# Transposes in place of matrix products with permutation matrices, in a stack of four graph layers

## The chip, the cores and the metric

The kernel runs on one core of a Trainium2 chip. The metric is the time of one execution on the device, in microseconds (us). TensorE multiplies matrices, VectorE (DVE in the profile), ScalarE (ACT) and GpSimd (POOL) work on what it leaves, and DMA engines move data between memory and the core. TensorE takes one operand as weights, loaded beforehand (PEld in the profile), streams the other one past it (PE), and writes to PSUM, from where DVE or ACT copies the result.

## The reference

Sixteen graphs with N = 1024 nodes and D = 256 features, all in fp32, pass through four layers. Each layer normalises its input, applies ReLU, runs one graph operation with the adjacency matrix and adds the result to its input:

```
h = relu(layernorm(x)); x = x + layer_0(h, adj)   # attention with mask adj
h = relu(layernorm(x)); x = x + layer_1(h, adj)   # normalised adjacency
h = relu(layernorm(x)); x = x + layer_2(h, adj)   # node by node, gated
h = relu(layernorm(x)); x = x + layer_3(h, adj)   # sum of neighbours, MLP
```

Layers 0, 1 and 3 are large products. Layer 2 is sequential: a scan over the nodes,

```
def step(h, i):
    x = h_e[:, i];  x_par = row_i(norm_adjT) @ h
    r, z = split(sigmoid(x @ W_ioux.T + b + x_par @ W_iouh.T + b'))
    hc = tanh(x @ W_coux.T + ... + (x_par * r) @ W_couh.T + ...)
    h[:, i] = z * x_par + (1 - z) * hc
```

so the value of node i depends on the new values of its neighbours with a smaller index.

## The kernel before

**Order.** Each graph's nodes are cut into NT = 8 blocks of P = 128. Within a block the kernel does not follow the nodes' own order. It looks for an order in which nodes that do not depend on one another stand together, in 8 groups of S = 16, and works on a group of all 16 graphs at once. What layer 2 reads must therefore be permuted, and most of it also transposed. Both happen in one product on TensorE: for a block of data A (128 by 128) and a permutation matrix `to`, the product of A as weights and `to` as the moving operand is A transposed, with its columns in the new order. `to` is made on VectorE by comparing the row `step` (0 to 127) with each node's `place` (L413, L600).

**Layers 0 and 1** run in one loop over the graphs (`layers_0_1`). The work of layer 0 on graph i, of layer 1 on graph i−1 and two kinds of side work are recorded side by side: the order of nodes (`orders`, on VectorE) and, from the tenth turn of the loop on, `put_in_order(b)` for one or two graphs a turn. The order in which each engine then takes the instructions is set by a scheduler, which works from its own costs of instructions. The sums of both layers are L290; their four results per layer are copied from PSUM at L293 and L295; the small products that follow are L360 and L391.

`put_in_order(b)` is a generator in six parts, and has all but one of the changed lines:

- It loads two diagonals of blocks of the adjacency (`ad`), a column of blocks (`ab`) and the layer's input (`h2`), makes `to`, and masks and scales `ad` and `ab` on GpSimd (L416 to L421).
- L429: 16 products (2 halves c of the features, 8 blocks t) turn `h2` into `hT`. Four of them fill one PSUM tile `pt` of 512 columns, of which there are two; ACT (c = 0, L432) or DVE (c = 1, L434) copies it out. Then `hT` goes to memory as `heT_d` (L436).
- L443 and L445: 15 products turn the blocks of `ad` into `ao`, which takes the same single buffer as `hT` (L438, name "hT"). Its copies (L450 on ACT, L452 on DVE) so wait until `heT_d` is written. L454 and L455 write `ao` to memory.
- L458 sums eight products with `ab` into `bs` (scaled at L460), and L464 turns its two halves, which L466 copies and L467 writes as `base_d`.

This makes 16 × (16 + 15 + 2) = 528 products with a permutation.

**Layer 2** has its order on TensorE, VectorE, ScalarE and GpSimd written out by hand. It goes through the blocks t and their 8 groups s. Each group takes one or more rounds (`round_`; K = `KS[s]` of them: 1, 1, 1, 1, 1, 2, 2, 4), a chain of products at L784, four transposes at L816 with the identity, and gates on ACT and DVE. Between the steps of that chain `fill` puts tasks for later groups and for the next block, by weights and costs written in the code. One of these is the sum over the other blocks (`task` in `base_tasks`, L616, copied and scaled on ACT at L603); at its end `turn` takes the sum, turns its two halves with `to` (L630) and copies them to `bxt` (L631). The planner's cost of `turn` is 0.44. It runs for 16 graphs and 7 blocks: 224 products. Its PSUM tile `pf` is one of three, which the tasks of L616, L666, L737 and L765 use too.

Two places use `nc.tensor.transpose` already: L816 and, in layer 3, L1118.

Of the kernel before, what the change touches and what calls it, by code (L numbers as in the profile page):

```python
# [16 lines left out]
P = 128  # L17
# [22 lines left out]
def gnn_stack(ctx: ExitStack, tc: tile.TileContext, a: dict, out: bass.AP):  # L40
    nc = tc.nc
# [29 lines left out]
    def rows(ap):  # L71
        return ap.rearrange("(t p) d -> p t d", p=P)
# [155 lines left out]
    def layers_0_1():  # L228
        with ExitStack() as st:
# [68 lines left out]
            at, q, g, h1, h2, dis = {}, {}, {}, {}, {}, {}  # L298
# [101 lines left out]
            def put_in_order(b):  # L400


                ad = big.tile([P, NT, 2 * P], F32, name="ad")
                nc.sync.dma_start(ad[:, 0, P:], a["adjT"][b, :P, :P])
                nc.sync.dma_start(ad[:, 1:], bass.AP(tensor=a["adjT"].tensor, offset=a["adjT"].offset + b * N * N + P * N,
                                                     ap=[[N, P], [P * N + P, NT - 1], [1, 2 * P]]))
                ab = big.tile([P, NT, P], F32, name="ab")
                nc.sync.dma_start(ab, rows(a["adj"][b])[:, :, :P])
                if b not in h2:
                    h2[b] = big.tile([P, NT, D], F32, name="h2", bufs=2)  # L410
                    nc.sync.dma_start(h2[b], rows(he_d[b]))
                to = big.tile([P, NT, P], F32, name="to")
                nc.vector.tensor_tensor(to, step[:, None].to_broadcast([P, NT, P]),  # L413
                                        place.rearrange("i (t b) -> i t b", b=B)[:, :, b : b + 1].to_broadcast([P, NT, P]),
                                        ALU.is_equal)
                nc.gpsimd.affine_select(out=ad[:, :, P:], in_=ad[:, :, P:], compare_op=ALU.is_gt, fill=0.0, base=0,  # L416
                                        pattern=[[0, NT], [-1, P]], channel_multiplier=1)
                nc.gpsimd.affine_select(out=ab[:, 0], in_=ab[:, 0], compare_op=ALU.is_ge, fill=0.0, base=0,
                                        pattern=[[-1, P]], channel_multiplier=1)
                nc.gpsimd.tensor_tensor(ad[:, :, P:], ad[:, :, P:], dinv[:, b][:, :, None].to_broadcast([P, NT, P]), ALU.mult)  # L420
                nc.gpsimd.tensor_tensor(ad[:, 1:, :P], ad[:, 1:, :P],  # L421
                                        dinv[:, b, 1:][:, :, None].to_broadcast([P, NT - 1, P]), ALU.mult)
                yield
                hT = big.tile([P, DC, N], F32, name="hT")
                for c in range(DC):
                    for t0 in range(0, NT, 4):
                        pt = psum.tile([P, 512], F32, name="pt")
                        for t in range(4):
                            nc.tensor.matmul(pt[:, t * P : (t + 1) * P], h2[b][:, t0 + t, c * P : (c + 1) * P], to[:, t0 + t],  # L429
                                             start=True, stop=True)  # L430
                        if c == 0:
                            nc.scalar.copy(hT[:, c, t0 * P : (t0 + 4) * P], pt)  # L432
                        else:
                            nc.vector.tensor_copy(hT[:, c, t0 * P : (t0 + 4) * P], pt)  # L434
                    if c == DC - 1:
                        nc.gpsimd.dma_start(heT_d[b], hT)  # L436
                    yield
                ao = big.tile([P, NT, 2 * P], F32, name="hT")  # L438
                nc.gpsimd.memset(ao[:, NT - 1, P : P + S], 0.0)
                for t0 in range(0, NT, 2):  # L440
                    pt = psum.tile([P, 2, 2, P], F32, name="pt")
                    for t in (t0, t0 + 1):
                        nc.tensor.matmul(pt[:, t - t0, 0], ad[:, t, P:], to[:, t], start=True, stop=True)  # L443
                        if t + 1 < NT:
                            nc.tensor.matmul(pt[:, t - t0, 1], ad[:, t + 1, :P], to[:, t + 1], start=True, stop=True)  # L445
                    n = 4 * P if t0 + 2 < NT else 3 * P
                    got = ao[:, t0 : t0 + 2].rearrange("p t n -> p (t n)")[:, :n]
                    pt = pt.rearrange("p t k n -> p (t k n)")[:, :n]
                    if t0 % 4 == 0:
                        nc.scalar.copy(got, pt)  # L450
                    else:
                        nc.vector.tensor_copy(got, pt)  # L452
                        yield
                nc.gpsimd.dma_start(near_d.rearrange("(t b j) n -> b j t n", t=NT, b=B)[b], ao[:, :, : P + S])  # L454
                nc.gpsimd.dma_start(next_d[b].rearrange("t j n -> j t n"), ao[:, : NT - 1, P + S :])  # L455
                pb = psum.tile([P, 512], F32, name="pt")
                for j in range(NT):
                    nc.tensor.matmul(pb[:, :D], ab[:, j], h2[b][:, j], start=j == 0, stop=j == NT - 1)  # L458
                bs = small.tile([P, D], F32, name="bo", bufs=1)
                nc.scalar.activation(bs, pb[:, :D], AF.Copy, scale=dinv[:, b, 0:1])  # L460
                yield
                pt = psum.tile([P, 512], F32, name="pt")
                for c in range(DC):
                    nc.tensor.matmul(pt[:, c * P : (c + 1) * P], bs[:, c * P : (c + 1) * P], to[:, 0], start=True, stop=True)  # L464
                bo = small.tile([P, DC, P], F32, name="bo", bufs=1)
                nc.vector.tensor_copy(bo, pt[:, :D].rearrange("p (c i) -> p c i", c=DC))  # L466
                nc.gpsimd.dma_start(base_d[b], bo)  # L467
                del h2[b]
                yield
# [10 lines left out]
            for i in range(B + 2):  # L480
# [3 lines left out]
                for b in when.get(i, ()):  # L484
                    if b < i - 2:
                        del h2[b]
                    job = put_in_order(b)
                    next(job)
                    jobs += [lambda job=job: next(job)] * 6
# [52 lines left out]
    def layer_2(shared, early):  # L542
        with ExitStack() as st:
# [32 lines left out]
            def base_tasks(t, bxt):  # L576
# [20 lines left out]
                def summed(b, pb):  # L597
                    if b not in state:
                        to = big.tile([P, P], F32, name="to")
                        nc.vector.tensor_scalar(to, step, place[:, t * B + b : t * B + b + 1], None, op0=ALU.is_equal)  # L600
                        state[b] = [to]
                        bs = big.tile([P, D], F32, name="bs")
                        nc.scalar.activation(bs, pb, AF.Copy, scale=dinv[:, b, t : t + 1])  # L603
                        state[b].append(bs)
# [19 lines left out]
                def turn(b, held):  # L624
                    def run():
                        summed(b, held[0])
                        to, bs = state.pop(b)
                        pt = psum.tile([P, DC, P], F32, name="pf", bufs=3)
                        for c in range(DC):
                            nc.tensor.matmul(pt[:, c], bs[:, c * P : (c + 1) * P], to, start=True, stop=True)  # L630
                        return lambda: nc.vector.tensor_copy(bxt[:, :, b], pt)  # L631
                    return 0.44, run

# [235 lines left out]
            with tc.manual_schedule(engines={mybir.EngineType.PE, mybir.EngineType.DVE, mybir.EngineType.Activation, mybir.EngineType.Pool}):  # L869
# [17 lines left out]
                for t in range(NT):  # L887
# [10 lines left out]
                    for s in range(NS):  # L898
# [36 lines left out]
                        for c in range(DC):  # L935
                            to = x[:, c].rearrange("p (b i) -> p b i", b=B)
# [282 lines left out]
```

## Time and profile before

| | |
|---|---|
| time, median of 3 runs | 4941.66 us (4936.22 to 4944.18) |
| span of the profiled execution | 4950.9 us |
| mean granted clock of TensorE | 0.978 |
| put_in_order runs in | 751 to 1545 us |
| layer 2 runs in | 1545 to about 3500 us, `turn` from 1592 to 3270 |
| layer 3's main part runs in | about 3500 to 4951 us |

The profile's page lists each engine's busy time first and then the costliest groups of instructions. In a group, "out<-in" names the tiles, "x512" counts the instructions, the two numbers after the bar are the busy time in us and the mean duration of one in ns, and what follows is the engine's idle time ahead of them and what ended it. Matmuls overlap in the pipeline, so the busy time of a group divided by its count, or the distance between starts in the timeline, tells more of their price than the mean duration. The products of the change in this trace:

| line | product | products | matmul instructions | PE busy, us |
|---|---|---|---|---|
| L429 | hT from h2 | 256 | 512 | 64.6 |
| L443 | ao from ad, own block | 128 | 256 | 54.1 |
| L445 | ao from ad, next block | 112 | 224 | 45.3 |
| L464 | base from bs | 32 | 64 | (median 275 ns each) |
| L630 | turn | 224 | 448 | 76.0 |

### The profile page before, as it was taken

To read this page: it belongs to the slowest core of one execution; us is meant where nothing else is said; L and a number is where in the kernel's file an instruction comes from. 1 tells how busy PE (TensorE), PEld (TensorE's weight loads), DVE (VectorE), ACT (ScalarE), POOL (GpSimd) and SP (SyncE) were. 2 spreads that over 40 slices of the span, in tenths; PEclk is the share of its full clock that TensorE was granted. 3 is DMA by queue.
4 is the path that set the end of the run, shared out by engine and by line. 5 is a ranking of instruction groups with operands and counts; after the bars stand their busy time and mean duration, and the time that the engine had idled before them with its cause. 6 is when DMAs were issued, how large, how long until landed. Compare 5 with 4: busy or idle time off the path is not lost. (4 is left out here: it accounts for less than half of the span.)

```text
span 4950.9 us, 52564 instructions
## 1 busy us (share of the span) xinstructions
PE 4624.2 (93%) x18431; PEld 3061.1 (62%) x18431; DVE 2388.3 (48%) x6366; ACT 1174.7 (24%) x2388; POOL 1597.7 (32%) x1883
## 2 busy tenths in 40 slices
PE   8998999999997999999999999998799999999999
PEld 4443455565555777777777777776365555555656
DVE  6667754446443454545454445454534434334343
ACT  1111112112111222222222222222222323223232
POOL 3122333334323323323232232332523424234232
PEclk9999999999998999999999999999899999999999
DMA  5333335454535443544343445330422222221200
GB/s 157 116 93 98 95 96 177 165 171 149 186 118 189 142 136 119 158 137 152 122 138 108 146 129 164 123 118 34 149 84 86 77 77 85 77 94 69 84 26 17
DMA packets 530500, 577.13 MB, mean 117 GB/s; under 512 B 41552, under 2 KB 438992, under 8 KB 527824
## 3 DMA queue, kind: packets, MB, share of 16 engines
q1 hardware_dynamic: 499056, 460.79, 29.3%
q0 software_dynamic: 31040, 111.44, 6.3%
q8 instruction: 195, 3.19, 0.3%
q14 instruction: 209, 1.71, 0.1%
HBM read 470.17 MB, written 116.65 MB: 119 GB/s over the span
## 5 line engine op out<-in xcount | busy, mean ns | idle before, releaser
L290 PE MATMUL pa<-at,h 128*128 128x512 f32 x1088 | 492.2, 604 | 29.4 <-DVE ag L295 29.4
L1094 PE MATMUL ph<-ag,w 128*128 128x512 f32 x1024 | 478.9, 611 | 33.9 <-DVE hh L1098 33.9
L1132 PE MATMUL po<-w,hh 128*128 128x256 f32 x2048 | 447.7, 379 | 0.0
L616 PE MATMUL pf<-hb,ab 128*128 128x256 f32 x1568 | 419.4, 387 | 22.0 <-ACT bs L603 18.8
L1132 PEld LDWEIGHTS po<-w,hh 128*128 128x128 f32 x2048 | 387.8, 190 | 59.3 <-issue 7.9
L290 PE MATMUL pa<-at,q 128*128 128x512 f32 x960 | 420.9, 594 | 0.0
L290 PEld LDWEIGHTS pa<-at,h 128*128 128x128 f32 x1088 | 207.9, 194 | 271.4 <-issue 229.3
L1094 PEld LDWEIGHTS ph<-ag,w 128*128 128x128 f32 x1024 | 179.1, 190 | 295.4 <-DVE hh L1098 151.7
L1100 POOL TENSOR_TENSOR ss<-ss,sq 128x512 f32<-128x512 f32 x224 | 302.3, 1349 | 121.8 <-ACT sq L1097 117.4
L983 POOL DMA_INDIRECT hs_d<-h,table x128 | 129.9, 1015 | 621.1 <-DVE gz L739 446.6
L616 PEld LDWEIGHTS pf<-hb,ab 128*128 128x128 f32 x1568 | 284.0, 194 | 73.7 <-ACT bs L603 26.0
L290 PEld LDWEIGHTS pa<-at,q 128*128 128x128 f32 x960 | 179.7, 190 | 224.8 <-issue 220.7
L737 PE MATMUL pf<-wx,hs 128*128 128x512 f32 x512 | 248.0, 626 | 30.8 <-POOL hs L720 25.1
L1098 DVE TENSOR_SCALAR hh<-ph,b 128x512 f32<-128x512 f32 x256 | 190.0, 746 | 154.6 <-ACT sq L1097 120.7
L1079 PE MATMUL pa<-bxt,h 128*128 128x512 f32 x512 | 227.9, 597 | 19.9 <-POOL bxt L1061 19.9
L765 PE MATMUL pf<-bd,h 128*128 128x384 f32 (+5 forms) x768 | 218.8, 373 | 27.1 <-DVE bxt L768 27.1
L827 DVE TENSOR_TENSOR r<-r,x 128x256 f32<-128x256 f32 x230 | 123.6, 559 | 232.7 <-ACT r L826 231.2
L1079 PE MATMUL pa<-at,h 128*128 128x512 f32 x512 | 228.8, 597 | 0.0
L1097 ACT ACTIVATE sq<-ph,b 128x512 f32<-128x512 f32 x224 | 153.4, 685 | 234.2 <-PE ph L1094 189.1
L1124 ACT ACTIVATE hh<-hh,rw 128x512 f32<-128x512 f32 x256 | 168.4, 712 | 138.7 <-DVE hh L1123 136.7
L1135 DVE TENSOR_TENSOR x<-x,po 128x256 f32<-128x256 f32 x120 | 50.4, 420 | 289.0 <-PE po L1132 288.9
L1079 PEld LDWEIGHTS pa<-bxt,h 128*128 128x128 f32 x512 | 97.3, 191 | 137.1 <-issue 115.1
(233 smaller groups left out, 7948.3 us busy)
## 6 DMA issues: line engine op xcount, KB each, us to landing
at<-in_adjT SPq DMA_DIRECT2D x64, 1024.0 KB
ab<-in_adj SPq DMA_DIRECT2D x128, 512.0 KB
bxt<-in_adjT SPq DMA_DIRECT2D x64, 512.0 KB
at<-in_adjT SPq DMA_DIRECT2D x64, 512.0 KB
ad<-in_adj SPq DMA_DIRECT2D x128, 128.0 KB
x_d<-x POOLq DMA_DIRECT2D x16, 1024.0 KB
he_d<-h POOLq DMA_DIRECT2D x16, 1024.0 KB, 9.0
heT_d<-hT POOLq DMA_DIRECT2D x16, 1024.0 KB
```

The source lines that it names most:

```text
L290: nc.tensor.matmul(pa, h[:, mt, c * P : (c + 1) * P], at[n0 // 512][:, mt], start=mt == 0, stop=mt == NT - 1)
L616: nc.tensor.matmul(pb, ab[:, jts[k]], hb[:, jts[k]], start=k == 0, stop=k == len(jts) - 1)
L737: nc.tensor.matmul(pg, self.hs[:, c, g * GR : (g + 1) * GR], wx[:, c, D:], start=c == 0, stop=c == DC - 1)
L765: nc.tensor.matmul(pf, h[:, g, c * P : (c + 1) * P], bd[:, g, b4 : b4 + 4, S : S + far], start=True, stop=True)
L983: nc.gpsimd.indirect_dma_start(out=hs_d[t][g][:, :], out_offset=row(1, g, t, s), in_=h[:, g], in_offset=None)
L1079: nc.tensor.matmul(pa, h[b][:, mt, c * P : (c + 1) * P], at[b][n0 // NH][:, mt], start=mt == 0, stop=mt == NT - 1)
L1094: nc.tensor.matmul(ph, w1[:, c, k * P : (k + 1) * P], ag[:, c, n0 : n0 + NH], start=c == 0, stop=c == DC - 1)
L1097: nc.scalar.activation(sq, ph, AF.Square, bias=b1[:, k : k + 1])
L1098: nc.vector.tensor_scalar(hh[:, k], ph, b1[:, k : k + 1], None, op0=ALU.add)
L1100: nc.gpsimd.tensor_tensor(ss, ss, sq, ALU.add)
L1124: nc.scalar.activation(hh[:, k], hh[:, k], AF.Silu, scale=rw[:, k : k + 1])
L1132: nc.tensor.matmul(po, hh[:, c, k * P : (k + 1) * P], w2[:, c], start=c == 0, stop=c == HC - 1)
```

## The change

In five places a product with a permutation matrix is written as a transpose that has the permutation matrix where the identity usually stands. Operands, tiles, copies and transfers stay. [...]

```diff
@@ put_in_order
                         for t in range(4):
-                            nc.tensor.matmul(pt[:, t * P : (t + 1) * P], h2[b][:, t0 + t, c * P : (c + 1) * P], to[:, t0 + t],
-                                             start=True, stop=True)
+                            nc.tensor.transpose(pt[:, t * P : (t + 1) * P], h2[b][:, t0 + t, c * P : (c + 1) * P], to[:, t0 + t])
...
-                        nc.tensor.matmul(pt[:, t - t0, 0], ad[:, t, P:], to[:, t], start=True, stop=True)
+                        nc.tensor.transpose(pt[:, t - t0, 0], ad[:, t, P:], to[:, t])
                         if t + 1 < NT:
-                            nc.tensor.matmul(pt[:, t - t0, 1], ad[:, t + 1, :P], to[:, t + 1], start=True, stop=True)
+                            nc.tensor.transpose(pt[:, t - t0, 1], ad[:, t + 1, :P], to[:, t + 1])
...
-                    nc.tensor.matmul(pt[:, c * P : (c + 1) * P], bs[:, c * P : (c + 1) * P], to[:, 0], start=True, stop=True)
+                    nc.tensor.transpose(pt[:, c * P : (c + 1) * P], bs[:, c * P : (c + 1) * P], to[:, 0])
@@ turn
-                            nc.tensor.matmul(pt[:, c], bs[:, c * P : (c + 1) * P], to, start=True, stop=True)
+                            nc.tensor.transpose(pt[:, c], bs[:, c * P : (c + 1) * P], to)
```

The first edit takes a line away, so the lines behind it have numbers smaller by one in the changed kernel.

## The prediction

> **What bounds the kernel now.** I read the shares of the engines first, then their busy time by stage, then the groups of instructions by shape, then the timeline around the changed products.
>
> ```profile
> PE 4624.2 (93%) x18431; PEld 3061.1 (62%) x18431; DVE 2388.3 (48%) x6366; ACT 1174.7 (24%) x2388; POOL 1597.7 (32%) x1883
> ```
>
> TensorE is busy for 93% of the span, no other engine for half of it, so TensorE time is what can be saved. By stage (columns: stretch, its length, then busy us of PE, PEld, DVE, ACT, POOL, the granted clock, the DMA share, GB/s):
>
> ```profile
> 751.00:1545.00 794.00, 744.66 (x3052) 461.97 (x3050) 377.54 (x1143) 149.50 (x296) 268.82 (x289) 0.98 0.48 159
> 1545.00:1590.00 45.00, 27.44 (x91) 16.95 (x92) 10.12 (x21) 8.37 (x16) 16.48 (x23) 0.77 0.97 289
> 1590.00:3270.00 1680.00, 1590.97 (x7869) 1288.67 (x7867) 795.72 (x1895) 424.01 (x993) 501.37 (x723) 0.99 0.43 137
> ```
>
> The 528 products of put_in_order lie in the first stretch (L429, L443, L445, L464), the 224 of turn in the third (L630). PE is busy for 94% and 95% there, DMA for less than half. The 45 us between them are bound by DMA and hold none of the products.
>
> The groups by shape carry the argument:
>
> ```profile
> L429 PE MATMUL pt<-to,h 128*128 128x128 f32 x512 | 64.6, 283 | 7.9 <-ACT h L282 4.4 <-ACT hT L432 3.6
> L630 PE MATMUL pf<-to,bs 128*128 128x128 f32 x448 | 76.0, 295 | 10.4 <-issue 4.6 <-ACT bs L603 4.4 <-DVE bxt L768 0.8
> L816 PE MATMUL pa<-ident,x 128*128 128x128 f32 x460 | 69.9, 275 | 0.0
> ```
>
> L429 stands for 256 products (16 matrices, 2 halves, 8 blocks) and shows 512 instructions: an fp32 product of this shape is **two passes**, each with its own weight load. L816, in round_, already is a transpose of the same shape and type: 4 per round, 115 rounds, 460 instructions, so **one pass**. The means (283 and 275 ns) look alike, but passes overlap; what counts is the distance from start to start:
>
> ```profile
> 756.31 0.39 PE L445 MATMUL pt<-to,ad 128*128 128x128 f32 x2
> 756.53 0.39 PE L443 MATMUL pt<-to,ad 128*128 128x128 f32 x2
> ...
> 757.65 0.39 PE L445 MATMUL pt<-to,ad 128*128 128x128 f32 x2
> 757.87 7.03 PE L290 MATMUL pa<-at,q 128*128 128x512 f32 x16
> ...
> 761.97 0.58 ACT L450 COPY hT<-pt 128x512 f32<-128x512 f32 x1 [7.15 <-DMA heT_d<-hT]
> ...
> 764.74 0.38 PE L443 MATMUL pt<-to,ad 128*128 128x128 f32 x2
> ```
>
> From 756.31 to 757.65 are 6 products: 0.223 us each. In layer 3 four transposes at L1118 take from 3574.24 to 3574.68:
>
> ```profile
> 3574.24 0.60 PE L1118 MATMUL pr<-ident,rms 128*128 128x128 f32 x4
> 3574.68 3.60 PE L1094 MATMUL ph<-ag,w 128*128 128x512 f32 x8
> ```
>
> That is 0.110 us each, and the matmul after them follows without a gap. L816's starts are 0.109 us apart as well.
>
> [...] the trace shows half the passes and 0.110 against 0.223 us, 2.0x, and I use that. [...] The trace shows bursts of 4 transposes at most and no drop with them, so it leaves this open for bursts of 8: a rival below. [...] all is fp32 here, so the copies that follow (0.58 us ACT, 0.69 us DVE in the timeline) stay as they are.
>
> **The change part by part.** Each product loses one matmul pass and one weight load: 0.223 − 0.110 = 0.113 us. I assume that a permutation as the moving operand costs what the identity costs; size and type are the same.
>
> *put_in_order, 528 products (256 + 240 + 32):* 528 × 0.113 = **59.7 us gross**. Off this come two things.
>
> First the buffer of hT. hT and ao share one buffer, so ao's first copies (L450, L452) wait until heT_d has been written; the waits of ACT and DVE on that transfer are long (the copy above waited 7.15 us). What TensorE has to do meanwhile hides it. Two PSUM banks (8 products) can be filled ahead; the third needs the copy. Before, between the last L429 (756.0) and the third bank (764.74) stand 8 products and 8 of L290's: 8.7 us. The copy was done at 761.97 + 0.58 = 762.55, 6.5 us after; so 2.2 us to spare. The changed program's TensorE order (the scheduler has moved L290's products between them) has 1 product of L290, 8 transposes, 6 of L290: 14 passes of 0.43 us and 8 × 0.11 = 6.9 us. The last hT copies queue up on DVE (banks every 0.44 us, 0.69 us a copy), so the landing comes 0.25 us later: 0.1 us to spare, about nothing. In the first 6 jobs the landing took the same 6 us and the wait stays near zero. Later transfers are slower, and TensorE did wait already (from the list of waits: us in sum, times, the longest):
>
> ```profile
> PE pt L443 <- ACT hT L450: 7.9, 4, 4.3
> PE pt L443 <- DVE hT L452: 7.4, 2, 4.1
> ```
>
> Those waits and a few just hidden grow by up to 2 us each: I take 10 us for the stage, with 2 and 28 (14 jobs × 2) as ends. What is queued behind the third bank is the rest of the order, L290's sums among it, so such a wait is fully on the path.
>
> Second the tail: the last matrix (33 products, 3.7 us) runs with nothing beside it in a chain of copies and transfers; there 2 us stay unused. While hT is turned, copies aren't outrun: 8 transposes (0.88 us), one L290 product (0.86 us), 8 more, against 0.6 us a copy on ACT with two banks. Net for the stage: 59.7 − 12 = **48 us**.
>
> *turn, 224 products in 112 calls:* 224 × 0.113 = **25.3 us gross**, 0.226 us a call. Where calls stand among far and base tasks with K=1 (about half), the next waits are for copies of what TensorE has just made, and these move with it. In the rounds of K=2 and 4, the call is the filler while ACT and DVE finish h:
>
> ```profile
> 2008.04 0.61 PE L630 MATMUL pf<-to,bs 128*128 128x128 f32 x4
> 2008.48 1.89 PE L616 MATMUL pf<-hb,ab 128*128 128x256 f32 x8
> 2010.21 1.05 PE L797 MATMUL pa<-ai,ho 128*128 128x128 f32 x8
> ```
>
> DVE ends the first half of ho at 2009.59 and the second at 2010.39 in that round. L797 could start at 2009.98, and its fifth pass, at 2010.43, needs the second half plus a weight load: some 0.1 us comes back as a wait. That is 28 calls × 0.11 = 3.1 us. In 7 calls of the first K=2 round the next task waits for DVE (L768 at 1985.12, queued behind L804) and in 7 at the end of K=4 for a copy on ACT: 14 × 0.226 = 3.2 us. Net: **19 us**. The planner's cost of 0.44 for the call isn't changed, and this part's order is written by hand, so nothing else moves.
>
> The weight loads that go cost nothing of their own, as they run beside the matmuls: their saving is within the 0.113 us. DMA moves the same bytes; 159 GB/s becomes 169 in the first stretch, far below the 289 of the next.
>
> Sum: 48 + 19 = 67 us; 4941.66 − 67 = **4875 us**.
>
> **The rivals.**
> 1. *All of it arrives*: 85 us, **4857 us**. For it: PE at 94%, and most waits move with TensorE. Against: the 0.1 us of room above.
> 2. *The transfer takes the place of the work removed*: each of 14 jobs waits 2 us more (28), half of turn's saving (13) is lost to DVE and ACT: 59.7 − 28 − 2 + 12 = 42 us, **4900 us**. For it: the waits on heT_d exist. Against: six of the early jobs land in 6 us sharp.
> 3. *The clock falls*. After 4.1 us of waiting at 1217.8 the trace shows a clock of 0.50 for 3.4 us:
>
> ```profile
> 1222.60:1226.00 3.40, 3.40 (x9) 2.10 (x8) 3.29 (x10) 0.00 (x0) 3.40 (x5) 0.50 0.25 42
> ```
>
> Such a drop costs 1.7 us. If transposes count as idle, 8 + 8 + 8 of them with single L290 products between are half idle for 3 us. Two drops for each of 16 jobs cost 54 us; with rival 2 the sum is 42 − 54 = −12 us: **4954 us, slower**. One drop a job: 42 − 27 = 15 us, 4927. Against: the real matmuls between, and shorter idle stretches, as the 1.39 us before 832.38, which no drop followed.
>
> **How the numbers follow.** Forecast, 55 to 78 us saved: 0.58. Rival 1, over 78: 0.12. Rival 2, 30 to 55: 0.20. Rival 3 and its half, and what I haven't seen: 0.10, of which 0.03 lie within 0.2% (9.9 us), 0.04 above, and 0.03 still faster. So faster 0.93, same 0.03, slower 0.04. The range: from 4850 (everything, with 6 us of present waits gone) to 4908, which takes in rival 2 with 8 us to spare.
>
> **What would show it.** L429, L442, L444, L463 and L629 of the changed kernel must show 256, 128, 112, 32 and 224 instructions, half of before, with starts 0.11 us apart; PE's busy time must fall by about 80 us. The stretch of put_in_order should shorten by about 48 us and layer 2 by about 19; layers 0 to 1 before 751 us and layer 3 not at all. Waits of PE for L449 or L451 (the ao copies) of more than 30 us in sum would speak for rival 2; a lower clock in the stretch from 751 us for rival 3. The prediction is wrong at its root if the products still take two passes.

## The result and the profile after

| | kernel before | changed kernel |
|---|---|---|
| time, median (range) | 4942.92 us (4936.22 to 4956.44, 4 runs) | 4866.77 us (4857.41 to 4875.50, 4 runs) |
| ratio | | 0.9842, 95% interval 0.9814 to 0.9870 |
| span of the profiled execution | 4950.9 us | 4855.7 us |
| mean granted clock in it | 0.978 | 0.981 |

The changed kernel is 76 us faster; 67 were forecast, 4875 us against 4867, inside the range of 4850 to 4908. A later series gave 4869.21 and a ratio of 0.9843 (0.9830 to 0.9856). The time of either kernel moves by up to 20 us from run to run with the clock that TensorE was granted (the kernel before: 4937.39 us at 0.981, 4959.19 us at 0.976), so profiles are compared below by stretch, with the clock in view. That is also why the two spans lie 95 us apart.

The page after, its row of engines:

```profile
PE 4521.4 (93%) x17679; PEld 2951.8 (61%) x17679; DVE 2381.2 (49%) x6366; ACT 1173.7 (24%) x2388; POOL 1602.6 (33%) x1883
```

752 matmuls and 752 weight loads fewer (18431 − 17679), 102.8 us less of busy PE; DVE and ACT as before. The groups by shape in the changed kernel:

```profile
L815 PE MATMUL pa<-ident,x 128*128 128x128 f32 x460 | 69.3, 273 | 0.0
L629 PE MATMUL pf<-to,bs 128*128 128x128 f32 x224 | 46.1, 288 | 10.1 <-DVE bxt L767 5.4 <-ACT bs L602 4.4
L429 PE MATMUL pt<-to,h 128*128 128x128 f32 x256 | 35.3, 281 | 3.8 <-DVE to L413 2.0 <-ACT hT L431 1.8
```

The counts are halved (L442, L444 and L463 have 128, 112 and 32): one pass for each product. The timeline of the first graph in put_in_order shows the price and the new order:

```profile
752.08 1.04 PE L429 MATMUL pt<-to,h 128*128 128x128 f32 x8
752.96 1.02 PE L290 MATMUL pa<-at,q 128*128 128x512 f32 x2
753.82 1.04 PE L429 MATMUL pt<-to,h 128*128 128x128 f32 x8
754.69 1.02 PE L290 MATMUL pa<-at,q 128*128 128x512 f32 x2
755.55 0.27 PE L442 MATMUL pt<-to,ad 128*128 128x128 f32 x1
755.66 0.27 PE L444 MATMUL pt<-to,ad 128*128 128x128 f32 x1
...
756.42 5.32 PE L290 MATMUL pa<-at,q 128*128 128x512 f32 x12
762.61 0.33 PE L442 MATMUL pt<-to,ad 128*128 128x128 f32 x1 [0.87 <-ACT hT L449]
```

Eight transposes from 752.08 to 752.96 are 0.11 us each: a permutation costs what the identity costs (0.109 us at L816, 0.110 at L1118 in the kernel before). At 762.61 TensorE has run out of other work and has waited 0.87 us for the copy of ao, which is the wait that the prediction put at nothing for the early graphs.

By stretch (put_in_order, then turn; first the kernel before, then the changed one):

```profile
752.25:1543.90 791.65, 743.21 (x3049) 461.43 (x3047) 377.12 (x1142) 149.50 (x296) 268.57 (x287) 0.98 0.48 158
1592.00:3269.70 1677.70, 1588.73 (x7861) 1287.33 (x7859) 793.77 (x1890) 423.71 (x993) 499.39 (x722) 0.99 0.43 137
```

```profile
752.10:1488.00 735.90, 682.29 (x2521) 394.92 (x2519) 367.44 (x1142) 147.94 (x296) 270.57 (x287) 0.97 0.53 171
1532.70:3180.20 1647.50, 1554.31 (x7636) 1248.29 (x7635) 797.99 (x1889) 423.75 (x992) 501.68 (x722) 0.99 0.43 139
```

Put_in_order lost 55.8 us and turn's stretch 30.2. The rest, 9 us, is before and behind turn's stretch (48.1 to 44.7 us, 239.7 to 233.7), where the change has nothing. Where the clock is at 0.5, TensorE's starts lie about twice as far apart: in the changed kernel 0.21 us for transposes from 1045.72 in place of 0.11, and 0.85 us for L290's products from 1047.01 in place of 0.43. So half of the time at 0.5 is put down to the clock here; this is an estimate from those distances, and a little high, as TensorE isn't always at work then. The clock was at 0.5 for 21 us less in these two parts, and half of that covers the 9 us. The trace's record of the clock gives 30.7 us at 0.5 in put_in_order before and 37.5 after, 47.8 and 20.5 us in turn's stretch. Without half of it the stretches take 776.2 and 717.1 us, 1653.8 and 1637.3 us: **put_in_order gave 59 us, turn 17**. This is called "at equal clock" below.

The same two stretches in all runs, from the first transpose or product of the one to the last of its kind, measured and without the clock's part:

| kernel | put_in_order, us | without clock | turn, us | without clock |
|---|---|---|---|---|
| before | 791.6 | 776.2 | 1677.7 | 1653.8 |
| changed | 735.9 | 717.1 | 1647.5 | 1637.3 |
| e6_change_again | 737.3 | 713.4 | 1644.1 | 1639.0 |
| e1_put_only | 734.3 | 713.8 | 1672.4 | 1655.3 |
| e2_turn_only | 787.0 | 775.0 | 1648.3 | 1636.4 |
| e3_halves | 740.7 | 720.3 | 1655.9 | 1637.1 |
| e4_turn_twice | 730.2 | 713.1 | 1672.4 | 1651.9 |
| e7_put_twice | 780.7 | 765.4 | 1649.6 | 1635.9 |
| e8_cost | 734.6 | 715.8 | 1652.3 | 1640.3 |
| e9_sum_between | 759.6 | 723.8 | 1651.2 | 1635.9 |
| e10_before_between | 798.4 | 776.3 | 1671.7 | 1652.9 |

Rows with the same code in a stretch agree within 4 us or so once the clock is out. Twice the difference of two columns is the time at 0.5. In put_in_order it is 24 to 31 us with two passes a product (before, e2, e7) and 34 to 48 with one (e9 and e10, which move other work, left out); in turn's stretch it is 34 to 48 us with two (before, e1, e4, e10) and 10 to 38 with one. With one profile for each kernel this is no more than a hint that the falls of the clock moved from the second stretch to the first.

Whole runs can be compared in the same way without a profile, since every run has its mean clock on record, to three digits. By the same estimate, time multiplied by clock is the time without the falls. Its mean is 4841.5 us for the kernel before (45 runs with a standard deviation of 3.0), 4764.5 for the changed one (9 runs), 4780.2 for e1_put_only (4) and 4822.8 for e2_turn_only (6). So the change gives 77 us in all, put_in_order alone 61 and turn alone 19.

### The profile page after: what moved, and what is told of

It reads as the page before. It is cut to its first block, busy times and chain, and to the rows that moved or that the text cites. A ratio compares the mean times of both kernels' runs of the same rounds, so it can differ in the third digit from the quotient of the medians.

```text
span 4855.7 us, 51055 instructions
## 1 busy us (share of the span) xinstructions
PE 4521.4 (93%) x17679; PEld 2951.8 (61%) x17679; DVE 2381.2 (49%) x6366; ACT 1173.7 (24%) x2388; POOL 1602.6 (33%) x1883
## 5 line engine op out<-in xcount | busy, mean ns | idle before, releaser
L290 PE MATMUL pa<-at,h 128*128 128x512 f32 x1088 | 490.2, 603 | 32.8 <-DVE ag L295 32.8
L290 PE MATMUL pa<-at,q 128*128 128x512 f32 x960 | 424.5, 595 | 0.0
L290 PEld LDWEIGHTS pa<-at,h 128*128 128x128 f32 x1088 | 207.6, 194 | 273.9 <-issue 228.1
L290 PEld LDWEIGHTS pa<-at,q 128*128 128x128 f32 x960 | 178.4, 190 | 215.8 <-issue 212.8
```

Of the source, the lines that this page charges most:

```text
L290: nc.tensor.matmul(pa, h[:, mt, c * P : (c + 1) * P], at[n0 // 512][:, mt], start=mt == 0, stop=mt == NT - 1)
```

## The experiments

The theory (A): a product with a permutation cost two passes and costs one now, 0.113 us less, and TensorE is so full in both places that most of it reaches the end. Its rivals: the transfer of hT takes back a good part (B), layer 2 is where the gain is (C), and transposes let the clock fall (rival 3 of the prediction).

**e1_put_only: only put_in_order is changed.**

```diff
-                            nc.tensor.transpose(pt[:, c], bs[:, c * P : (c + 1) * P], to)
+                            nc.tensor.matmul(pt[:, c], bs[:, c * P : (c + 1) * P], to, start=True, stop=True)
```

> Only put_in_order's 528 products are transposes; turn multiplies as before. Theory A (a product costs one pass less, 0.113 us, and nearly all of it reaches the end): 528 x 0.113 = 60 us less about 3 us of new waits for the hT transfer, so 55 to 60 us under the kernel before, about 4886 us. Theory B (as predicted: 10 us go to the transfer of hT and 2 to the tail): 48 us under, about 4895 us. Theory C (the gain of layer 2 is the larger part, as the stretch of turn shrank by 30 us in the profile): 45 us under or less.

Measured: 4882.11 us, ratio 0.9866 (0.9850 to 0.9883) to 4946.47, so 66 us. The stretch of put_in_order is 62 us shorter at equal clock, that of turn unchanged (1653.8 and 1655.3). The interval, 58 to 74 us, holds theory A's upper end; B's 48 and C's 45 are out, as they are for the 61 us that whole runs give without the clock.

**e2_turn_only: only turn is changed**, the kernel before with this one edit:

```diff
-                            nc.tensor.matmul(pt[:, c], bs[:, c * P : (c + 1) * P], to, start=True, stop=True)
+                            nc.tensor.transpose(pt[:, c], bs[:, c * P : (c + 1) * P], to)
```

> Only turn's 224 products are transposes; put_in_order multiplies as before. Theory A: the stretch of turn lost 30 us in the profile, of which 14 were a difference in the clock, so 16 to 20 us under the kernel before, about 4925 us. Theory B (as predicted): 19 us. Theory C (shorter turns also let the clock fall less often): 27 us or more under, about 4915 us. With e1 it must add up to the whole change, 76 us, if the two parts do not touch each other.

Measured: 4920.67 us, ratio 0.9949 (0.9936 to 0.9962), 25 us with an interval from 19 to 32. This interval holds all three theories. The stretch itself is 17 us shorter at equal clock (1653.8 to 1636.4), as in the changed kernel, which is A's number and close to B's. The other 8 us are mostly clock: time multiplied by clock gives 19 us for the same runs. The parts, 66 and 25, add up to 91 where 78 were measured for both; at equal clock they add up, 62 and 17 in the stretches against 59 to 63 and 15 to 17, and 61 and 19 in whole runs against 77. Whether shorter turns let the clock fall less often, as C has it, stays open: the table above hints at it, and the changed kernel as a whole doesn't show it.

**e4_turn_twice: every transpose of turn done twice.**

```diff
-                            nc.tensor.transpose(pt[:, c], bs[:, c * P : (c + 1) * P], to)
+                            for _ in range(2):
+                                nc.tensor.transpose(pt[:, c], bs[:, c * P : (c + 1) * P], to)
```

> The changed kernel with each transpose of turn done twice in a row (the same result): 224 more passes of 0.109 us, 24 us of TensorE time. Where TensorE sets the time of layer 2, the kernel becomes 20 to 24 us slower than the changed one, about 4889 us. If a quarter of turn's time lies beside waits for other engines, as the prediction has it, 18 us. If turn is mostly hidden, under 8 us.

Measured: 4880.45 us, ratio 0.9863 (0.9846 to 0.9880); 11 us over the changed kernel's 4869.21 of the other series, 13 to 15 us in the stretch at equal clock. None of the three numbers of the expectation was met: this lies between the 8 us of "mostly hidden" and the 18 of the prediction. Of 24 us of passes about half are on the path, not three quarters.

**e7_put_twice: every transpose of put_in_order done twice**, so that a product has two passes again. The scheduler counts them and sets TensorE's order nearly as in the kernel before: of the stretch's 2520 matmul instructions, a product with a permutation counted once, 2460 come in the same order in the two traces, and 2169 in those of the kernel before and the changed one (the other three such lines likewise):

```diff
+                            for _ in range(2):
                                 nc.tensor.transpose(pt[:, t * P : (t + 1) * P], h2[b][:, t0 + t, c * P : (c + 1) * P], to[:, t0 + t])
```

> The changed kernel with each of put_in_order's 528 transposes done twice in a row (the same result): again two passes for each product, and the order on TensorE goes back to nearly that of the kernel before. Theory A (the number of passes alone makes the gain): the time of the kernel with turn alone changed, about 4921 us, 53 to 60 us over the changed kernel. If the gain came from the new order as well, it lies under 4911 us or over 4931 us.

Measured: 4913.42 us, ratio 0.9930 (0.9918 to 0.9942). That is 44 us over the changed kernel and 7 under e2_turn_only, less than theory A said; time multiplied by clock gives 51 and 8. In the stretch, 765.4 us at equal clock against 775.0 of e2_turn_only. The waits of TensorE in that stretch say where the 10 us are. In e2_turn_only (us in sum, times, the longest):

```profile
PE pt L443 <- ACT hT L450: 8.2, 4, 4.2
PE pt L443 <- DVE hT L452: 7.3, 2, 4.1
PE pmm L360 <- DVE x L361: 6.3, 4, 3.5
```

and in e7_put_twice:

```profile
PE pt L444 <- ACT hT L452: 8.0, 4, 4.2
...
PE pt L444 <- DVE hT L454: 3.2, 1, 3.2
```

The wait of L360 is gone from its list, and 4 us of the wait for ao's copies. PE's busy time is the same (741.0 and 741.1 us), of which 3 us would be expected to go, as 1056 passes start 0.109 us apart and not 0.112 (e5_burst), and are hidden by a lower clock: from the table, 30.6 us at 0.5 in place of 24.0. So passes make most of put_in_order's gain (48 to 52 us of 59 to 63, from e7_put_twice to the rows with one pass), and some 10 us go with the scheduler's order and the slightly shorter pass. No run had the old order with one pass, so the order's part is a difference and not a measurement of its own.

**e3_halves: hT and ao in two buffers of half the size.** The shape of the edit, which cuts the two transfers of ao into halves as well, so that a graph has three more transfers and not two:

```diff
-                hT = big.tile([P, DC, N], F32, name="hT")
                 for c in range(DC):
+                    hT = big.tile([P, N], F32, name="hT", bufs=2)
...
-                    if c == DC - 1:
-                        nc.gpsimd.dma_start(heT_d[b], hT)
+                    nc.gpsimd.dma_start(heT_d[b, :, c], hT)
...
+                    if t0 % 4 == 0:
+                        ao = big.tile([P, NT // 2, 2 * P], F32, name="hT", bufs=2)
```

> The changed kernel with hT and ao cut in two halves that take turns in two buffers of half the size: the first half of hT is sent as soon as it is full, and the copies of ao's first half wait for that transfer alone, which begins about 2 us earlier. Theory A: the waits of TensorE for the copies of ao (22 us in sum in the changed kernel's profile) mostly go, and 5 to 15 us with them: about 4857 us. Theory B's rival (the transfer was hidden, the waits come from elsewhere): within 5 us of the changed kernel, or slower, as two more transfers per graph are issued on GpSimd.

Measured: 4867.50 us, ratio 0.9835 (0.9820 to 0.9850): the changed kernel's time, as the rival had it. The list of waits in the stretch, first of the changed kernel, then of the halves:

```profile
PE pt L442 <- ACT hT L449: 13.2, 6, 3.7
...
PE pt L442 <- POOL ad L420: 5.6, 3, 3.3
PE pt L442 <- DVE hT L451: 5.2, 2, 3.9
PE pt L442 <- POOL x L380: 4.1, 1, 4.1
PE pt L442 <- POOL hT L438: 4.0, 1, 4.0
```

```profile
PE pt L443 <- POOL ad L420: 13.9, 8, 4.1
...
PE pt L429 <- DVE to L413: 8.7, 1, 8.7
PE pt L443 <- ACT hT L450: 8.6, 4, 2.7
```

The 22 us of the expectation counted the 4.0 us put down to L438 as a wait for the transfer. It wasn't one: the transposes that waited (at 1279.98) are the first of their graph and need `ad`, whose scaling (L420) ended at 1279.93, and the small L438 merely came next on GpSimd. The waits on the copies of ao alone fell from 18 us to 9, and others came in their place: GpSimd isn't done with the masks and scales of `ad` (L420; 14 us in place of 10 with the 4.0, and GpSimd has 293 us of work in the stretch in place of 271), and once the comparison that makes `to` came 8.7 us late. Where the transfer was the last to end, it was not by much.

**e9_sum_between and e10_before_between: more work behind the transfer.** The sum over `ab` moves from behind ao to between hT and ao (the same move in both kernels):

```diff
+                pb = psum.tile([P, 512], F32, name="pt")
+                for j in range(NT):
+                    nc.tensor.matmul(pb[:, :D], ab[:, j], h2[b][:, j], start=j == 0, stop=j == NT - 1)
+                bs = small.tile([P, D], F32, name="bo", bufs=1)
+                nc.scalar.activation(bs, pb[:, :D], AF.Copy, scale=dinv[:, b, 0:1])
+                yield
                 ao = big.tile([P, NT, 2 * P], F32, name="hT")
...
-                pb = psum.tile([P, 512], F32, name="pt")
```

> The changed kernel with put_in_order's sum over ab (8 products, 3.5 us of TensorE, which need neither hT nor ao) moved from behind ao to between hT and ao. TensorE has then 11 us of work in place of 6.9 between the last transpose of hT and ao's third bank, so the transfer of hT lands behind it. Unlike the halves, nothing is needed earlier than before, so the masks of ad should not take the wait's place. Theory A: the 22 us of waits for ao's copies mostly go, and with them some falls of the clock: 10 to 20 us under the changed kernel, about 4854 us. If other waits take their place as with the halves: within 5 us of 4869 us.

> The same move in the kernel before (products, no transposes). There the waits for ao's copies were 16 us. Theory A: 8 to 15 us under the kernel before, less than the move gives the changed kernel, since the change had taken some of the work that hid the transfer. Rival: nothing in either.

Measured: 4888.14 us for the changed kernel with the move, ratio 0.9880 (0.9864 to 0.9895), 19 us slower than without; 4950.74 us for the kernel before, ratio 1.0006 (0.9999 to 1.0013). Both expectations were wrong. In the waits of e9_sum_between a line stands first that is hardly there in the changed kernel (1.8 us):

```profile
PE pt L429 <- ACT hT L431: 19.5, 8, 4.9
PE pt L448 <- DVE hT L457: 14.5, 3, 5.7
```

and ACT's own list has what the copies of hT wait for:

```profile
ACT hT L431 <- DMA next_d<-hT: 37.1, 7, 9.4
```

hT and ao share one buffer in turn, so there are two transfers in each round of it: hT out before ao may come in, and ao out before the next graph's hT. Delaying ao hid a good part of the first and uncovered the second. ScalarE's copies of ao had waited 89.9 us for `heT_d` in the changed kernel and wait 6.9 here, while those of hT wait 37.1 us for `next_d` in place of 9.0. TensorE's own waits that the landing of `heT_d` ended are 8.9 us (4.1 and 4.8) in place of 13.2. The other two waits for L457 (5.7 and 4.0 us) have to do with neither transfer: the copy started on VectorE without idle time behind L323, which ran 4.4 us in the first case. Part of the 19 us is the clock, which fell behind the longer waits (71.7 us at 0.5 in the stretch against 37.5); 7 to 10 us are left at equal clock. In e10_before_between TensorE's waits for the copies of hT rose from 3.6 to 10.1 us as well, and the 8.2 us of L360 went, so nothing was left of either.

**e5_burst: does the clock take transposes for idle time?** Behind the last layer of the changed kernel, on a tile of its own: 160 products, 320 transposes, 80 products, then 20 times 8 transposes and 4 products.

```diff
+        for k in range(320):
+            nc.tensor.transpose(pt[:, k % 4 * P : (k % 4 + 1) * P], step, ident)
```

> The changed kernel with a tail behind the last layer, on a PSUM tile that nothing else uses: 160 products 128x128 (36 us), 320 transposes of the same tile (35 us), 80 products (18 us), and 160 transposes with 4 products after each 8 (36 us). It asks whether the clock takes transposes for idle time. Theory A (a transpose is busy time for the clock, no fall within bursts of 8 in the changed kernel): the clock stays at 1.0 in all parts, starts 0.109 us apart, about 125 us more. Rival 3 (it counts as idle): the clock falls to 0.5 some us into the 320 transposes and they take up to 70 us; in the last part, where products are half of the time, it may stay up.

Measured, by the four parts (columns as before, the clock third from the end):

```profile
4867.00:4902.80 35.80, 35.73 (x320) 35.73 (x321) 0.02 (x1) 0.00 (x0) 0.93 (x1) 1.00 0.08 31
4902.80:4937.80 35.00, 35.00 (x323) 35.00 (x322) 0.00 (x0) 0.00 (x0) 0.00 (x0) 1.00 0.00 1
4937.80:4955.70 17.90, 17.90 (x162) 17.90 (x161) 0.00 (x0) 0.00 (x0) 0.00 (x0) 1.00 0.01 2
4955.70:4991.00 35.30, 35.30 (x322) 35.30 (x320) 0.00 (x0) 0.00 (x0) 0.00 (x0) 1.00 0.00 1
```

The clock stays at 1.00 through 35 us of nothing but transposes, which start 0.109 us apart, as it does through the 35.8 us of products ahead of them. The kernel takes 4994.67 us, 125 more than e6_change_again, as theory A had it. Rival 3 is out for these fp32 transposes. Where the changed kernel's clock does fall in put_in_order, an idle stretch came first, as the 3.44 us for L449 ahead of 1045.46, from where transposes start 0.21 us apart. In the 3.4 us ahead of each of its eight falls there TensorE was busy for 1.6 us at most.

**e6_change_again and e8_cost.** The changed kernel once more in the second series, and the same with the planner's cost of turn halved:

```diff
-                    return 0.44, run
+                    return 0.22, run
```

> The changed kernel once more, beside the others of this call: 4860 to 4875 us, 72 to 82 us under the kernel before. Where its parts alone gave 66 us (put_in_order) and 25 us (turn), 91 in sum, the difference from 78 is either the spread of the clock (then this run lies at the upper end) or waits that the two parts share.

> The changed kernel with the planner's cost of turn in layer 2 set from 0.44 to 0.22, which is what it now takes. Theory A: the tasks shift by part of a step between the fills of a round, and the waits of layer 2 for r (9 us in the profile of the changed kernel, 6 before) fall back: 0 to 5 us faster than the changed kernel. Rival: the tasks are as coarse as before, nothing to be measured, within 5 us.

Measured: 4869.21 us, ratio 0.9843 (0.9830 to 0.9856), and 4868.17 us, ratio 0.9842 (0.9828 to 0.9855). The change holds at 78 us. The cost makes no difference that can be measured: the wait for r, which was to fall back to 6 us, is 8.1 in e8_cost and 9.3 in e6_change_again. Why was not looked into further. No version of these is faster than the changed kernel beyond doubt.

## Why the prediction was right, step by step

- *Two passes become one, 0.223 to 0.110 us.* Right, to the count of instructions and 0.109 to 0.11 us; the permutation costs what the identity costs. PE's busy time was to fall by about 80 us and fell by 102.8. Busy time at 0.5 holds the longer distances between starts (0.21 us in place of 0.11 from 1045.72 on), and the changed profile has 34 us less at 0.5 in all (182.2 in place of 216.1); without half of that the fall is about 86 us (an estimate, as if TensorE had been busy in all of it).
- *Put_in_order gives 48 us.* Too little: 59 to 63 at equal clock, 56 in the raw profile. The term mis-sized is the 12 us taken off for the transfer and the tail. TensorE's waits ahead of ao's products rose from 20.0 us to 32.1, and only one part of that is what the prediction described. Sorted by what ended them, read from the timeline at each wait:

| what ended the wait | before, us | after, us |
|---|---|---|
| `heT_d` landed, then a copy of ao | 6.3 | 13.2 |
| a copy of ao that stood behind other work on its engine | 9.0 | 5.2 |
| the masks and scales of `ad` on GpSimd (L420) | 4.4 | 9.6 |
| a late copy of hT on VectorE | 0 | 4.1 |
| put down to L439, not sorted | 0.3 | 0 |

  The first row is the wait of the prediction: 7 us more, where 10 were taken. But its two lines of waits (7.9 and 7.4 us) were not all of this kind. The 7.4 us are two waits of 4.1 and 3.3 us in which the copy stood behind L323 on VectorE (it started at 1221.17 and 1320.59, without idle time behind L323), and 1.6 of the 7.9 are the same with L282 on ScalarE. The third and fourth rows it did not have. They include the 4.0 us put down to L438 and the 4.1 put down to L380 in the list under e3_halves; the latter ended at 1178.91, when VectorE had copied hT (L433).

  Nor did I cost the new order by anything but the transfer. The scheduler that put L290's products between the transposes also put them between L360's (in the first such place runs of 10, 8 and 8 passes, with L290 between them, where runs of 12 and 16 stood), and these waits fell:

```profile
PE pmm L360 <- DVE x L361: 8.2, 4, 3.5
...
PE pt L443 <- POOL ad L420: 4.4, 1, 4.4
PE pt L429 <- ACT h L282: 4.4, 1, 4.4
```

  are lines before, the first and the last of them those that fell; after, the first is

```profile
PE pmm L360 <- DVE x L361: 1.4, 2, 0.8
```

  and the last isn't in the list. That is 11 us back against the 12 us on ao's products, and a few smaller waits grew (L290 for DVE from 5.6 to 9.0). PE's idle time in the stretch was 48.4 us before (791.65 − 743.21) and 53.6 after, so of the 12 us that the prediction took off only 5 were lost. That the new order brought these waits down is read from the two traces; e7_put_twice, in which L360's wait also went with nearly the old order, shows only that small shifts of order move such waits.
- *The wait stays near zero in the first 6 jobs.* Nearly: 0.87, 0.84 and 0.86 us in the first, third and fifth. What failed is the landing. In the first job it came at 761.97 in both kernels, though hT was ready and its transfer issued 1.0 us earlier (756.30 in place of 757.32): the transfer took 5.6 us in place of 4.6. What held it isn't known.
- *Turn gives 19 us.* Nearly: 15 to 17 in the stretch at equal clock, 19 in whole runs of e2_turn_only. The calls named as lost were lost. In all seven of the first round of K=2, the distance from the call to the next task was 0.92 us and stays so (the lines are the second of them), and in the seven at the end of K=4 it was 0.91 to 1.00 us and stays so too:

```profile
1921.83 0.38 PE L629 MATMUL pf<-to,bs 128*128 128x128 f32 x2
1922.75 0.43 PE L764 MATMUL pf<-bd,h 128*128 128x64 f32 x2 [0.54 <-DVE bxt L767]
```

  In the calls ahead of L796, its 8 passes take 1.18 us in place of 1.05 (from 1947.35, and much the same in the 20 others that the trace shows whole), 0.13 us where 0.11 were put. What was missing is the wait for r in the rounds, from 5.7 us to 9.2 (7.2 in e1_put_only, where turn is as before).
- *Rival 2, the transfer takes the place of the work removed.* Out as a sum, present as a mechanism: the waits that the transfer ended grew by 7 us and not by 28, and those for L449 and L451 are 18 us where more than 30 were to speak for it. Neither way of easing the transfer brought anything, e3_halves nor e9_sum_between, since GpSimd's masks, or the second transfer of the same buffer, ended right behind it.
- *Rival 3, the clock.* Out by e5_burst. I had left it open for lack of a burst in the trace. The sign that the prediction named for it did appear, a lower clock in the stretch from 751 us (0.97 in place of 0.98, 37.5 us at 0.5 in place of 30.7), but these falls follow waits and not transposes (the 3.4 us ahead of each held 1.6 us of busy TensorE at most).
- *Rival 1, all of it arrives*, 85 us: nearer than I gave it credit for in put_in_order, wrong in turn.

That the sum came within 10 us is in part luck: put_in_order was 11 to 15 us too low and turn up to 4 too high, so the errors partly cancelled, and within put_in_order waits that the prediction did not have went up and down by as much as the one that it had.

What stays open: whether the change itself shifts the falls of the clock, since no run held the clock still, and what the scheduler's order is worth alone.

## What to carry to other kernels

A product of fp32 data with a permutation matrix is a transpose with that matrix as its moving operand: here half the passes and weight loads (752 of each in place of 1504), the same copies behind it. Count the instructions of a group against the products in the source, and take the distance between starts, not the duration, whose median was 273 to 275 ns for either form here. Where a scheduler sets the order, read the list of all waits around the change, not only the one that the change touches: here the order that it found cost 12 us ahead of ao's products and gave back 11 on others. Read behind each wait, too, what the copy it names was itself waiting for: more than half of the 15.3 us of waits "for the copies of ao" before the change were a copy's place in its engine's queue, and no transfer.

## What the runs showed of the hardware that I had not expected

The clock stayed at 1.00 through 35 us of fp32 transposes (e5_burst). In that unbroken stretch they started every 0.109 us, and the fp32 products ahead of them every 0.112 us a pass.

In put_in_order of the changed kernel the long waits of TensorE came with falls of the clock: each of the seven waits of 3.3 us or more ahead of ao's products met one, to 0.5 for 3.41, 6.83 or 10.24 us, which costs up to 1.7 us for each 3.4, an estimate from the starts that lie twice as far apart there. Waits of up to 2.3 us earlier in the stretch met none. The length of the wait isn't all of it: TensorE was idle for 2.60 us from 1204.7 in the kernel before, and no fall followed, while 1.70 us from 1467.5 and 2.18 us from 1472.6 in the changed kernel were followed by one. In the traces of these two kernels TensorE was busy for 1.9 us at most in the 3.41 us ahead of each of the 71 falls.
